# Row scatters of a routed layer: tied by dependences of the transfer in place of waiting GpSimd copies

## The chip, the cores and the metric

The kernel runs on one core of a Trainium2 chip. The metric is the device time of one execution in microseconds: the median of three timed runs before the change is 793.06 us (792.67 to 793.94). A separate, profiled execution shows where the time lies.

Names: PE is TensorE (PEld its weight loads), DVE VectorE, ACT ScalarE, POOL GpSimd, SP SyncE. L634 is line 634 of the kernel before.

## What is computed

The input x has 32 sequences of 256 rows of 128 numbers, all float32. The layer is `x + attention(norm(x)) + experts(norm(x))`:

- attention with 16 heads of 8 numbers, rotated queries and keys, a causal window of 64 positions, softmax, and an output projection;
- a router with 8 experts that keeps two per row with softmaxed weights; each expert is 128 to 512 with gelu, then 512 back to 128.

```
scores = where(j <= i and i - j <= 64, q @ k.T / sqrt(8), -inf)
y = softmax(scores) @ v;  attn = y @ Wproj.T + bproj
weights, indices = top_k(xn @ gate_w.T + gate_b, 2); weights = softmax(weights)
out += w_e * (gelu(xn @ w1[e] + b1[e]) @ w2[e] + b2[e])     for each expert e
return x + attn + out
```

## The kernel before

The order of every engine is the order in which the program is written: all engines are under a manual schedule (L133), and a helper turns data dependences into semaphore waits.

**Attention** runs over 32 sequences z, each in four rounds r = 0 to 3 (L811). A round makes one tile of transposed scores for sequence z on one buffer (`high`, L612: mask matmuls L622, then score matmuls L634) and one tile of the other orientation for an earlier sequence on another buffer (`less`, L681: masks L689, scores L703). VectorE takes the row maxima of the first (mx, L648). ScalarE takes exponentials of the second (pr, L713). Both buffers exist once, so the masks of the next round wait for the maximum and for the exponential. Behind that each round has a job of its own:

- r = 0: values of sequence z - 2 (y, L725), transposed out by VectorE (yt, L734); the parts of the maxima of z - 1 are turned (L672) and copied by ScalarE (L677);
- r = 1: a projection of queries or keys (L549), which VectorE shuffles and multiplies (L558, L565) and GpSimd multiplies for the rotation (L564); the two are added by VectorE two or three rounds later (L571);
- r = 2: more values (L725, L734), the division (L752, L754) and the transpose yT (L760);
- r = 3: the maxima are split into three bfloat16 parts (pc, L659 to L662), v is projected (L589), and the sequence z - 2 ends with the output projection and its addition to x (L774).

**Beside** it a generator (L1037) is advanced once a round by `turn` (L805). It normalises the rows of later sequences (`norm`, L259: statistics on VectorE, the power on GpSimd L274, which is written at the end of the round by `flush`, then the scaling by ScalarE), routes four groups of 16 row tiles (`route`, L306), and writes the row scatters: for each of the 64 tiles of 128 rows and each of the two chosen experts, one indirect DMA from GpSimd that puts 128 rows of 130 numbers (128 values, the row's number and its weight) into the experts' space xs_d in DRAM (`spread_tile`, L454, the DMA at L457). A round has two scatters. `numbers` (L448) writes the row's number and weight into four tiles at a time.

Ahead of each scatter stands a copy of one number on GpSimd (L1079). What it copies is taken from the list `past`, to which the round's VectorE results are appended: the maximum first (L649), then pc (L664), yt (L738), yT (L762) or the sum x (L775). The even scatter's copy reads `past[0]`, the maximum; the odd one's reads `past[-1]`, the last of them. `turn` empties the list (L809). The scatters are declared free of each other (`apart`, L465).

**The experts** (L909) begin when all scatters are written. Attention stands still in between: 71 blocks of 256 rows are loaded by SP (L922 to L932), turned, multiplied up (L952), put through gelu (L958), multiplied down (L970), weighted (L975, L976) and scattered back by GpSimd (L981), each of these scatters with a memset of one number behind it (L988). Then the last ten sequences run through attention while GpSimd adds the experts' rows (L1028).

Of the kernel before, what the change touches and what calls it, by code (L numbers as in the profile page):

```python
# [15 lines left out]
ALU = mybir.AluOpType  # L16
AX = mybir.AxisListType
# [12 lines left out]
NT = TB // P  # L30
# [66 lines left out]
def tile_layer(  # L97
# [16 lines left out]
    nc = tc.nc  # L114
# [12 lines left out]
    def kept(name, shape, dtype=F32):  # L127
        return keep.tile(shape, dtype, tag=name, name=name)
# [18 lines left out]
    xns = [xnp.tile([P, NT, ROW], F32, tag=f"xn{u}", name=f"xn{u}") for u in range(NU)]  # L147
# [43 lines left out]
    xs_d = tc.dram_tile([NE * ER + NI * BT, ROW], F32, name="xs_d")  # L191
# [14 lines left out]
    slot = kept("slot", [P, NN, 2], I32)  # L206
# [238 lines left out]
    spread, returned = [], []  # L445
    gap = kept("gap", [1, 1])

    def numbers(u, k):  # L448

        nc.gpsimd.tensor_copy(  # L450
            xns[u][:, :, D:].bitcast(I32), goes[:, k, u * NT : (u + 1) * NT, :]
        )

    def spread_tile(n, k):  # L454

        spread.append(
            nc.gpsimd.indirect_dma_start(  # L457
                out=xs_d,
                out_offset=bass.IndirectOffsetOnAxis(ap=slot[:, n, k : k + 1], axis=0),
                in_=xns[n // NT][:, n % NT, :],  # L460
                in_offset=None,
            )
        )

    def apart(transfers, name):  # L465

        transfers = [t.ins for t in transfers]
        for t in transfers:
            tc.add_to_no_dep_group(name, t)
        for t in transfers:  # L470
            tc.declare_no_dep(t, group=name, reason="rows of their own")


    class Attention:
# [137 lines left out]
        def high(self, z, m, ip):  # L612

            q, km = self.qk[z // 2, 0][:, z % 2, :], self.kms[z % 3]
            ps = self.ps_s.tile([P, 2, 4, P], F32, tag="sh", name=f"sh{z}_{m}{ip}")

            def masks():
                for ii in range(2):
                    half = slice(HB * ii, HB * ii + HB)
                    for h in range(2):  # L620
                        which = 0 if m == 0 and h == 0 else 1
                        nc.tensor.matmul(  # L622
                            ps[HB * h : HB * h + HB, ii, :, :],
                            lhsT=unit2[half, :],
                            rhs=mq[half, which, :].unsqueeze(1).to_broadcast([HB, 4, 2 * HB]),
                            start=True, stop=False, skip_group_check=True,
                        )

            def scores():
                for h in range(2):  # L630
                    t = 2 * m + h
                    for ii in range(2):
                        r = slice(32 * (2 * ip + ii), 32 * (2 * ip + ii) + 32)
                        nc.tensor.matmul(  # L634
                            ps[HB * h : HB * h + HB, ii, :, :],
                            lhsT=q[r, t * HB : (t + 1) * HB],
                            rhs=km[r, :, t * HB : (t + 2) * HB],
                            start=False, stop=True, skip_group_check=True,
                        )
                        yield  # L640

            def drain():
                if (m, ip) == (0, 0):
                    self.seqs[z] = dict(
                        mx=self.work.tile([P, 2, 4, 4], F32, tag="mx", name=f"mx{z}")
                    )
                mx = self.seqs[z]["mx"][:, m, 2 * ip : 2 * ip + 2, :]
                nc.vector.tensor_reduce(mx, ps, AX.X, ALU.max, negate=True)  # L648
                self.past.append(mx[0:1, 0, 0:1])  # L649

            return masks, scores, drain

        def parts(self, z):

            mx = self.seqs[z]["mx"]
            pc = self.work.tile([P, 2, 4, 4, 3], BF16, tag="pc", name=f"pc{z}")
            at = [pc[:, :, :, :, n].rearrange("p m s i -> p m i s") for n in range(3)]
            rest = self.work.tile([P, 2, 4, 4], F32, tag="rest", name=f"rest{z}")
            nc.vector.tensor_copy(at[0], mx)  # L659
            nc.vector.tensor_sub(rest, mx, at[0])  # L660
            nc.vector.tensor_copy(at[1], rest)
            nc.vector.tensor_sub(at[2], rest, at[1])  # L662
            self.seqs[z]["pc"] = pc
            self.past.append(pc[0:1, 0, 0, 0, 2:3])  # L664

        def parts_rows(self, z, both=False):

# [50 lines left out]
        def values(self, z, n):  # L718

            q = self.seqs[z]  # L720
            py = self.ps_y.tile([P, 4, P], F32, tag="y", name=f"y{z}_{n}")
            for tile_, lo, hi in ((0, 0, P),) if n == 0 else ((2, 0, HB), (1, HB, P)):
                for o in range(2):
                    for i in range(4):
                        nc.tensor.matmul(  # L725
                            py[32 * i : 32 * i + 32, 2 * o : 2 * o + 2, lo:hi],
                            lhsT=self.vsts[z % 3][:, tile_, i, o, :],
                            rhs=q["pr", n, i // 2][:, i % 2, 2 * o : 2 * o + 2, lo:hi],
                            start=True, stop=True, skip_group_check=True,
                        )  # L730

            if n == 0:
                q["yt"] = self.work.tile([P, 4, 8, 32], F32, tag="yt", name=f"yt{z}", bufs=1)
            nc.vector.transpose(  # L734
                q["yt"][:, :, 4 * n : 4 * n + 4, :].rearrange("p s n k -> p s (n k)"), py
            )
            if n == 0:
                self.past.append(q["yt"][0:1, 0, 0, 0:1])  # L738

        def divide(self, z):  # L740

            flat = self.seqs[z]["yt"].rearrange("p s n k -> p (s n k)")
            step = flat.ap[-1][0]

            def view(at, ap):
                return bass.AP(
                    tensor=flat.tensor, offset=flat.offset + at * step,
                    ap=[flat.ap[0]] + [[x * step, y] for x, y in ap],
                )

            rc = self.work.tile([P, 4, 8], F32, tag="rc", name=f"rc{z}")
            nc.vector.reciprocal(rc, view(30, [(248, 4), (32, 8)]))  # L752
            yn = self.work.tile([P, 8, 4, HD], F32, tag="yn", name=f"yn{z}", bufs=1)
            nc.vector.tensor_mul(  # L754
                yn.rearrange("p n s d -> p s n d"),
                view(0, [(264, 4), (32, 8), (1, HD)]),
                rc.unsqueeze(3).to_broadcast([P, 4, 8, HD]),
            )
            yT = self.work.tile([P, T], F32, tag="yT", name=f"yT{z}")
            nc.vector.transpose(yT, yn.rearrange("p n s d -> p (n s d)"))  # L760
            self.seqs[z]["yT"] = yT
            self.past.append(yT[0:1, 0:1])  # L762

        def end(self, z):

            u, b, yT = z // 2, z % 2, self.seqs.pop(z)["yT"]
            po = self.misc(f"pj{z}")
            for n in range(2):
                nc.tensor.matmul(
                    po[:, n * D : (n + 1) * D], lhsT=yT[:, n * P : (n + 1) * P], rhs=wpT,  # L770
                    start=True, stop=True,
                )
            xb = xs[u][:, 2 * b : 2 * b + 2, :]
            nc.vector.tensor_add(xb, po[:, 0 : 2 * D].rearrange("p (n d) -> p n d", d=D), xb)  # L774
            self.past.append(xb[0:1, 0, 0:1])  # L775
            self.ended.add(z)
            if u in self.added:
                self.out(z)
# [85 lines left out]
    att = Attention(list(range(NU)), (work, ps_m, ps_y, ps_s, fixed))  # L864
# [172 lines left out]
    def beside():  # L1037
# [32 lines left out]
        def scatters():  # L1070
            for g in range(NG):
                while g not in slots:
                    yield
                for n in range(2 * GN):
                    k, tile_ = n // GN, g * GN + n % GN
                    if n % NT == 0:
                        numbers(tile_ // NT, k)

                    nc.gpsimd.tensor_copy(gap, att.past[0] if n % 2 == 0 else att.past[-1])  # L1079
                    spread_tile(tile_, k)  # L1080
                    if n % 2:
                        yield

# [8 lines left out]
        def go_on(entry):  # L1092
            entry[2] = next(entry[1], None)
            if entry[2] is None:
# [7 lines left out]
                out=xs_d[rows : rows + NI * BT, :].rearrange("(j p n) d -> p j n d", p=P, n=2),  # L1102
                in_=void[:, 0:NI],
# [3 lines left out]
        u, g, last = 2, 0, False  # L1107
        while next(transfers, transfers) is not transfers:
# [25 lines left out]
            if len(slots) == NG and not last:  # L1134
                begin("blocks", blocks(rt, misc))
                last = True
# [46 lines left out]
```

## Time and profile before

| | |
|---|---|
| median of the timed runs | 793.06 us |
| the profiled execution | 838.41 us, span 836.6 us |
| granted TensorE clock, mean | 0.976 |
| PE, PEld | 750.3 us (90%), 483.2 us (58%) |
| DVE, ACT, POOL | 497.0 us (59%), 381.9 us (46%), 412.0 us (49%) |
| scatters L457 | 128, 126.5 us on POOL, 988 ns each, from 87.9 to 387.3 us |
| copies L1079 | 128 (of mx 80, yt 16, x 16, yT 16), 26.4 us |
| maxima L648 | 128, 156.3 us on DVE, 1221 ns each |
| exponentials L713 | 128, 130.8 us on ACT, 1022 ns each |
| expert scatters L981, memsets L988 | 142 each, 137.3 us and 12.6 us on POOL |

How to read it: busy times are those of one profiled execution. A group's row gives its line, engine, operation and tiles, then busy time and mean duration, then the idle time of its engine just before it and what ended most of that. A row of the waits gives who waited for whom, the total in us, how often, and the longest. In a timeline row the start and duration stand first, and in brackets the idle time before it and its releaser. The ends of matmuls are modelled. By time the execution has four stretches: start and first sequences (to 87 us), attention with scatters (to 387), experts (401 to 673), and the rest of attention (to the end).

### The profile page before, as it was taken

To read this page: it belongs to the slowest core of one execution; us is meant where nothing else is said; L and a number is where in the kernel's file an instruction comes from. 1 tells how busy PE (TensorE), PEld (TensorE's weight loads), DVE (VectorE), ACT (ScalarE), POOL (GpSimd) and SP (SyncE) were. 2 spreads that over 40 slices of the span, in tenths; PEclk is the share of its full clock that TensorE was granted. 3 is DMA by queue.
4 is the path that set the end of the run, shared out by engine and by line. 5 is a ranking of instruction groups with operands and counts; after the bars stand their busy time and mean duration, and the time that the engine had idled before them with its cause. 6 is when DMAs were issued, how large, how long until landed. Compare 5 with 4: busy or idle time off the path is not lost.

```text
span 836.6 us, 20453 instructions
## 1 busy us (share of the span) xinstructions
PE 750.3 (90%) x7524; PEld 483.2 (58%) x7524; DVE 497.0 (59%) x1163; ACT 381.9 (46%) x695; POOL 412.0 (49%) x668
## 2 busy tenths in 40 slices
PE   4899899888888889788999999999999989999985
PEld 2334444444444444333889998999899944444442
DVE  4658867887786687657233333333333348888763
ACT  4346455455455444434434344343344435454552
POOL 2301666477667644664355555555555553634300
PEclk9999999999999999989999999999999999999997
DMA  4600111111111111213677878887778634446100
GB/s 143 179 20 14 46 46 40 46 43 43 49 43 55 50 34 40 96 53 95 199 214 217 224 209 226 227 226 220 219 225 237 198 108 139 137 126 168 41 22 13
DMA packets 126372, 98.87 MB, mean 118 GB/s; under 512 B 14648, under 2 KB 112600, under 8 KB 126272
## 3 DMA queue, kind: packets, MB, share of 16 engines
q1 hardware_dynamic: 117344, 79.64, 34.3%
q0 software_dynamic: 8640, 17.84, 6.1%
q8 instruction: 60, 0.98, 0.5%
q14 instruction: 40, 0.33, 0.1%
q10 hardware_dynamic: 288, 0.08, 0.0%
HBM read 65.09 MB, written 24.02 MB: 107 GB/s over the span
## 4 chain that ended last, share of the span: by engine, by line
PE 63%; ACT 10%; DVE 9%; SPq 7%; issue 6%; DMA 4%; POOL 1%; ACTq 0%; DVEq 0%; POOLq 0%
PE sl L703 10%; PE ph L952 9%; PE po L970 9%; ACT pr L713 9%; PE sl L689 8%; PE sh L634 7%; PE y L725 6%; PE sh L622 5%; DVE mx L648 3%; DMA xg<-xs_d 2%; PE pm L672 2%; PE pk L549 1%; PE pq L549 1%; SPq L932 1%; PE pg L295 1%
## 5 line engine op out<-in xcount | busy, mean ns | idle before, releaser
L713 ACT ACTIVATE pr<-sl 128x1024 f32<-128x1024 f32 x128 | 130.8, 1022 | 232.2 <-PE sh L634 174.2
L648 DVE TENSOR_REDUCE mx<-sh 128x8 f32<-128x1024 f32 x128 | 156.3, 1221 | 106.0 <-PE sh L634 84.7
L981 POOL DMA_INDIRECT ys_d<-yg,at x142 | 137.3, 967 | 138.8 <-DVE yg L976 105.8
L958 ACT ACTIVATE h<-ph,b_b 128x256 f32<-128x256 f32 x284 | 116.3, 470 | 154.6 <-PE ph L952 141.6
L634 PE MATMUL sh<-km,rq 32*64 32x512 f32 x1024 | 153.4, 661 | 0.0
L457 POOL DMA_INDIRECT xs_d<-xn,slot x128 | 126.5, 988 | 44.3 <-issue 27.4
L703 PE MATMUL sl<-qm,rk 32*64 32x256 f32 (+1 forms) x1280 | 147.0, 502 | 0.0
L970 PEld LDWEIGHTS po<-w,h 128*128 128x128 f32 x1136 | 137.9, 192 | 4.3 <-issue 0.7
L970 PE MATMUL po<-w,h 128*128 128x128 f32 x1136 | 138.3, 275 | 0.6 <-issue 0.6
L952 PE MATMUL ph<-xgT,w 128*128 128x256 f32 x568 | 136.2, 383 | 1.1 <-DVE xgT L940 0.9
L689 PE MATMUL sl<-rs,pick_i 76*64 76x512 bf16 x512 | 81.9, 396 | 49.3 <-ACT pr L713 43.6
L952 PEld LDWEIGHTS ph<-xgT,w 128*128 128x128 f32 x568 | 103.3, 192 | 13.0 <-DVE xgT L940 1.1
L975 DVE TENSOR_TENSOR yg<-po,b 128x256 f32<-128x256 f32 x71 | 30.1, 424 | 112.1 <-PE pxg L938 66.4
L725 PE MATMUL y<-pr,vst 128*32 128x128 f32 (+1 forms) x1536 | 78.7, 331 | 2.8 <-issue 1.6
L689 PEld LDWEIGHTS <-pick_i 76*64 76x64 bf16 x512 | 27.8, 109 | 82.8 <-issue 71.2
L725 PEld LDWEIGHTS y<-pr,vst 128*32 128x32 f32 x1536 | 44.8, 117 | 53.3 <-issue 47.4
L703 PEld LDWEIGHTS sl<-qm,rk 32*64 32x64 f32 x1280 | 48.2, 134 | 39.2 <-issue 31.1
L677 ACT COPY rs<-pm 12x1024 bf16<-12x1024 bf16 x63 | 60.2, 1000 | 8.5 <-PE pm L672 7.9
L622 PE MATMUL sh<-mq,unit 64*64 64x512 bf16 x512 | 54.8, 417 | 3.5 <-DVE mx L648 3.2
L734 DVE STREAM_TRANSPOSE yt<-y 128x512 f32<-128x512 f32 x64 | 45.3, 708 | 10.5 <-PE y L725 9.0
L942 DVE COPY at<-xg 128x4 int32<-128x4 int32 x71 | 13.4, 189 | 62.7 <-issue 48.6
L622 PEld LDWEIGHTS <-unit 64*64 64x64 bf16 x512 | 15.7, 105 | 57.5 <-issue 57.2
(143 smaller groups left out, 840.3 us busy)
## 6 DMA issues: line engine op xcount, KB each, us to landing
w<-in_L_ffn_w_dram SPq DMA_DIRECT2D x142, 256.0 KB
xg<-xs_d SPq DMA_DIRECT2D x71, 130.0 KB
yc<-ys_d SPq DMA_DIRECT2D x32, 256.0 KB
b<-b_d SPq DMA_DIRECT2D x71, 64.0 KB
qm<-rq SPq DMA_DIRECT2D x128, 32.0 KB
out_dram<-x SPq DMA_DIRECT2D x32, 128.0 KB
km<-rk SPq DMA_DIRECT2D x126, 32.0 KB
x<-in_L_attn_x_dram SPq DMA_DIRECT2D x15, 256.0 KB
```

Source lines behind the costliest of these rows:

```text
L457: nc.gpsimd.indirect_dma_start(out=xs_d, out_offset=bass.IndirectOffsetOnAxis(ap=slot[:, n, k : k + 1], axis=0), in_=xns[n // NT][:, n % N ...
L622: nc.tensor.matmul(ps[HB * h : HB * h + HB, ii, :, :], lhsT=unit2[half, :], rhs=mq[half, which, :].unsqueeze(1).to_broadcast([HB, 4, 2 * HB]),
L634: nc.tensor.matmul(ps[HB * h : HB * h + HB, ii, :, :], lhsT=q[r, t * HB : (t + 1) * HB], rhs=km[r, :, t * HB : (t + 2) * HB], start=False, ...
L648: nc.vector.tensor_reduce(mx, ps, AX.X, ALU.max, negate=True)
L689: nc.tensor.matmul(ps[HB * e : HB * e + HB, ii, :, :], lhsT=pick_i[:, 2 * ip + ii, :], rhs=rs[e][:, :, n * P : (n + 1) * P], start=True, s ...
L703: nc.tensor.matmul(ps[HB * e : HB * e + HB, ii, :, lo:hi], lhsT=k[r, kt * HB : (kt + 1) * HB], rhs=qm[r, :, n * P + lo : n * P + hi], star ...
L713: nc.scalar.activation(pr, ps, AF.Exp, scale=1.0 / math.sqrt(HD))
L725: nc.tensor.matmul(py[32 * i : 32 * i + 32, 2 * o : 2 * o + 2, lo:hi], lhsT=self.vsts[z % 3][:, tile_, i, o, :], rhs=q["pr", n, i // 2][:, ...
L952: nc.tensor.matmul(ph[:, j * BT : (j + 1) * BT], lhsT=a[:, (k + j) * P : (k + j + 1) * P], rhs=xT, start=True, stop=True,)
L958: nc.scalar.activation(h[:, k + j, :], ph[:, j * BT : (j + 1) * BT], AF.Gelu, bias=b1_b[:, k + j, b : b + 1],)
L970: nc.tensor.matmul(po[:, n, :], lhsT=h[:, k, n * P : (n + 1) * P], rhs=z[:, k, :], start=(k == 0), stop=(k == NHC - 1),)
L981: nc.gpsimd.indirect_dma_start(out=ys_d, out_offset=bass.IndirectOffsetOnAxis(ap=at[:, n, 0:1], axis=0), in_=y[:, n, :], in_offset=None,)
```

## The change

The copies L1079 are gone. `spread_tile` is given an instruction, and the scatter gets a dependence on it with a semaphore, so that the DMA instruction itself waits. `past` now holds two instructions: the round's last score matmul (h and ii both 1) and its maximum. The even scatter waits for the first, the odd one for the second. The other entries of `past` are dropped. Behind each scatter GpSimd now sets one number to zero, as it does behind the experts' scatters.

On TensorE, ScalarE and SP the instructions, their order and their waits are the same as before; on VectorE three of the maxima no longer wait for GpSimd, and nothing else differs. On GpSimd each copy ahead of a scatter becomes a memset behind it, and the order of all else is the same.

```diff
-    def spread_tile(n, k):
+    def spread_tile(n, k, behind):
 
-        spread.append(
-            nc.gpsimd.indirect_dma_start(
...
+        t = nc.gpsimd.indirect_dma_start(
+            out=xs_d,
+            out_offset=bass.IndirectOffsetOnAxis(ap=slot[:, n, k : k + 1], axis=0),
+            in_=xns[n // NT][:, n % NT, :],
+            in_offset=None,
+        )
+        tc.add_manual_dep(
+            t.ins, behind.ins.name,
+            mybir.DependencyInfo(mybir.DependencyClass.Sync, mybir.DependencyReason.DATA),
+            reason="apart",
+        )
+        spread.append(t)
+        nc.gpsimd.memset(gap, 0.0)
...
-                        nc.tensor.matmul(
+                        last = nc.tensor.matmul(
                             ps[HB * h : HB * h + HB, ii, :, :],
...
+                        if (h, ii) == (1, 1):
+                            self.past.append(last)
                         yield
...
-                nc.vector.tensor_reduce(mx, ps, AX.X, ALU.max, negate=True)
-                self.past.append(mx[0:1, 0, 0:1])
+                self.past.append(nc.vector.tensor_reduce(mx, ps, AX.X, ALU.max, negate=True))
...
-            self.past.append(pc[0:1, 0, 0, 0, 2:3])
...
-            if n == 0:
-                self.past.append(q["yt"][0:1, 0, 0, 0:1])
...
-            self.past.append(yT[0:1, 0:1])
...
-            self.past.append(xb[0:1, 0, 0:1])
...
-                    nc.gpsimd.tensor_copy(gap, att.past[0] if n % 2 == 0 else att.past[-1])
-                    spread_tile(tile_, k)
+                    spread_tile(tile_, k, att.past[n % 2])
```

More of the change, by code (lines that the diff above doesn't have):

```diff
@@ L452, in numbers @@
         )
-    def spread_tile(n, k):
-        spread.append(
[L457 to L462, printed above, removed]
-        )
+    def spread_tile(n, k, behind):
[4 more added lines that the diff above has]
+            in_offset=None,
+        )
+        tc.add_manual_dep(
[5 more added lines that the diff above has]
+        nc.gpsimd.memset(gap, 0.0)
     def apart(transfers, name):
```

## The prediction

> **What bounds the kernel now.** I read the page first, then the stretches, then the waits inside the stretch that the change touches. The 128 row scatters run from 87.9 to 387.3 us, so the table of stretches is cut there, with the experts and the attention rounds behind them for comparison. The columns are length, then busy time of PE, weight loads, DVE, ACT and POOL, then clock, DMA share and GB/s.
>
> ```profile
> 87.00:386.00 299.00, 260.09 (x3167) 127.29 (x3163) 223.05 (x521) 144.47 (x229) 190.43 (x315) 0.96 0.15 48
> 401.00:673.00 272.00, 264.88 (x1819) 247.38 (x1820) 95.64 (x278) 116.83 (x284) 145.43 (x276) 1.00 0.76 216
> 690.00:810.00 120.00, 113.10 (x1526) 52.46 (x1524) 95.81 (x156) 59.99 (x81) 47.12 (x37) 1.00 0.38 109
> ```
>
> The experts are bound by TensorE (264.9 of 272 us). The rounds behind them take 120.4/36 = 3.34 us each (from one maximum L648 to the next). The scatter stretch holds 71 rounds in 299 us, 4.21 us each. No engine is full there, so it is a chain of hand-overs. Its waits:
>
> ```profile
> ACT pr L713 <- PE sh L634: 91.5, 43, 3.7
> ...
> DVE mx L648 <- PE sh L634: 43.1, 38, 3.1
> POOL gap L1079 <- DVE mx L648: 37.4, 32, 3.4
> ...
> POOL xs_d L457 <- issue: 27.2, 86, 1.9
> ```
>
> GpSimd waits for the maxima, as the copies demand. ScalarE and VectorE wait for scores, and the timeline shows a part of this that isn't arithmetic. First a round with a scatter, then the same kind of round after the experts:
>
> ```profile
> 252.31 0.59 PE L634 MATMUL sh<-km,rq 32*64 32x512 f32 x1
> 252.34 0.96 POOL L457 DMA_INDIRECT xs_d<-xn,slot  x1 [0.16 <-issue]
> ...
> 253.88 1.23 DVE L648 TENSOR_REDUCE mx<-sh 128x8 f32<-128x1024 f32 x1 [1.34 <-PE sh L634]
> ```
>
> ```profile
> 722.64 0.59 PE L634 MATMUL sh<-km,rq 32*64 32x512 f32 x1
> ...
> 723.33 1.22 DVE L648 TENSOR_REDUCE mx<-sh 128x8 f32<-128x1024 f32 x1 [0.93 <-PE sh L634]
> ```
>
> The last score ends at 252.90 and the maximum starts at 253.88, 0.98 us later, with a scatter running from 252.34 to 253.30. Without a scatter the gap is 723.33 - 723.23 = 0.10. I worked out this lag (start of the maximum less the later of last score's end and VectorE's being free) for all 128 rounds. With a scatter beginning or running around the score's end: 57 rounds, mean 0.67, together 38.0 us. Without: 0.07 (31 rounds) and 0.11 (40 rounds after the experts). The excess is 57 x (0.67 - 0.09) = 33 us, all in this stretch. Hand-overs from VectorE and ScalarE back to TensorE show no such lag.
>
> **How the profiled run stands to the median.** It took 838.4 us (span 836.6), the timed runs 793.1: 45.3 us less. The experts can't shrink by that (TensorE is busy 97%), nor the rounds after them (94%). So most of it must lie in the scatter stretch: 299 - 45 = 254 us, 3.58 a round. Thirteen rounds before and inside that stretch which have norms or routing but no scatter take 3.52; 71 of those are 250 us. Of the 49 us by which the profiled stretch exceeds that, the timed run can then have about 4, a twelfth. This is the number on which I choose: the hold-up is mostly a matter of the profiled execution.
>
> [...] I take the twelfth that the 45 us leave: -2.7 us, bounds 0 and -33.
>
> **The change part by part.** Profile columns: count, busy us, mean ns, then idle time before and its cause.
>
> ```profile
> L457 POOL DMA_INDIRECT xs_d<-xn,slot x127 | 125.5, 988 | 44.2 <-issue 27.2 <-POOL gap L1079 10.6 <-DVE pc L661 1.7
> L1079 POOL COPY gap<-mx 1x1 f32<-1x1 f32 x80 | 17.6, 220 | 38.4 <-DVE mx L648 37.4 <-issue 0.5
> ```
>
> - Removed: 128 copies L1079 (26.4 us on the page) and most of the 44.2 us between a copy and its scatter. Added: 128 memsets at the 88 ns that the same memset behind the expert scatters has (L988): 11.3 us. A scatter behind such a memset starts 0.22 us after it there, and one that waits for VectorE 0.28 us after the result: 128 x 0.25 = 32. GpSimd's use of the stretch is now 190 busy + 44 = 234 us, and after 190 - 26 + 11 + 32 = 207. In the profiled stretch of 299 that is all cover; in 254 us it is 92% before and 81% after. What queues behind a waiting scatter are the rotation products (L564), the power for the norms (L274) and the numbers (L450). VectorE waits for the first two only 0.5 us here, 0 in most rounds. In the tighter timed stretch, 11 norms could each wait up to 1 us: bounds 0 and -11, and since the trace shows almost none I take -1.0.
> - Moved: the even scatter waits for the last score on TensorE instead of the maximum. It now starts a median 0.88 us behind the end of the maximum, some 2.2 us after the score; it will start about 0.3 us after it. The odd one waits for the maximum rather than for the round's last VectorE result; its start goes from a median 2.33 us behind the maximum to some 0.3, if the even one (0.97 us) has ended. Both end some 2.6 us after the score, and the next score ends at 3.3 at the earliest. So maxima and exponentials should no longer be held: that is the -2.7 above. Each wait on GpSimd ends no later than now, so nothing queued behind it gets later.
> - The order on TensorE, VectorE, ScalarE and SP stays as it is; only three maxima lose a wait for GpSimd, which costs nothing today. SP's loads of rows wait for the last scatter: today it ends 387.28 and the first load is issued 388.96. The scatter can end 1.9 us earlier, but SP is itself busy with L580 to 387.2 and then reads two registers, some 1.4 us as between the later loads: -0.3.
> - [...] The even scatter now lies on the reduction, which is good, but in every fourth round the odd one lands on the casts L659 and L661. Rows: the reduction takes 1.22 us with or without a scatter; L659 takes 0.24 us without, 0.30 mean and 0.41 at most with one (8 of 18 have one now). [...] By the row, 8 more casts cost 0.06 to 0.18 each: +0.5, bounds 0 and +2.9.
>
> Sum: -2.7 - 1.0 - 0.3 + 0.5 = -3.5, so 789.5 us. In the profiled execution the whole 33 us are at stake. Against them stand results of values and projections which now meet a scatter: the transposes of y that did so had a lag of 0.25 us (8 cases); 48 rounds x 0.25 = +12. That gives 838.4 - 33 + 12 = about 817 profiled, a far larger fall than in the median.
>
> **Rivals.**
> 1. Slower: the hold-up moves rather than goes. The two scatters fill the 2.6 us behind each score, in which TensorE hands y to L734 and a projection to the rotation (three rounds in four, 48 in all), and VectorE works in order, so a late transpose delays the next maximum. If the hold reaches through both scatters, a transpose starts at about 3.05 instead of 1.3 us: 48 x 1.75 = 84 us against the 33 saved, +51 profiled and, by the twelfth, +4.3 timed: 797, up to 802 if more of it is real. It decides from 33/48 = 0.69 us a hand-over on. For it: the lag of 0.67 for maxima, and holds through two scatters in a row (257.08 to 259.00). Against: y's own rows had 0.25.
> 2. No change: GpSimd's room covers all of it and the timed runs have no hold: 793.0. For it: 45 against 49 us; VectorE almost never waits for GpSimd.
> 3. The hold is real in timed runs and the 45 us lie elsewhere: 33 - 12 = 21 us off, 772. Against: no other stretch has 45 us to give.
> 4. The scatters don't start where they are tied, because GpSimd is still at a rotation (1.27 us) or a power (1.05): then part of them lies as now; it ends between 2 and the forecast.
>
> **How the numbers follow.** Small gain (789.5, 786 to 791.4): 0.38. Rival 1: 0.33. Rivals 2 and 4 (no change): 0.17. Rival 3: 0.12. A difference under 0.2% (1.6 us) can't be told from none. Faster 0.50, same 0.17, slower 0.33. The range runs from 775 (most of rival 3 left out) to 802 (the end of rival 1).
>
> **What would show it.** Right: no L1079 copies; even scatters starting 0.3 us after the last L634; lags of the maxima under 0.2 us in scatter rounds; rounds near 3.8 us; a profiled span near 817 with a median that moves little. Rival 1: L734 and L558 starting 0.7 us or more late behind y and the projections, with TensorE's masks waiting for later maxima. Rival 3: a median falling as much as the span. Wrong altogether: a waiting scatter that costs GpSimd more than 0.3 us each, so that L571 or L278 waits for it.

## The result, and the profile after

The changed kernel takes 803.85 us (median of 11 runs, 798.78 to 811.05), the kernel before 793.06 (11 runs beside it). The two medians by themselves give 1.0136; the recorded ratio, from which one slow run of the changed kernel (811.05 us, at a clock of 0.973) is left out, is 1.0103, 95% interval 1.0075 to 1.0131: **slower by 1.0%**, where a gain of 0.5% was forecast, and above the range of 775 to 802. The changed kernel was run again as an anchor beside later experiments; that gave 1.0097 [1.0073, 1.012], 1.0186 [1.012, 1.0253] and 1.0121 [1.0062, 1.0179].

The profiled execution took 804.07 us (span 802.3, clock 0.982), so this time the profile and the timed runs agree. The kernel before was profiled once more as well (the first experiment): 796.16 us, span 793.4. That execution, and not the one of 838 us, is the partner for a comparison. The stretches of the changed kernel, then those of that second profile of before (columns as above; each first row is about the scatter stretch, the second lies within the experts):

```profile
87.00:365.00 278.00, 256.49 (x3184) 127.30 (x3174) 236.41 (x522) 144.15 (x230) 176.37 (x317) 0.96 0.16 52
380.00:650.00 270.00, 268.19 (x1909) 249.87 (x1907) 97.37 (x280) 118.90 (x284) 148.23 (x284) 1.00 0.76 219
```

```profile
87.00:356.00 269.00, 251.37 (x3168) 124.33 (x3165) 225.60 (x522) 144.48 (x230) 193.50 (x316) 0.97 0.17 54
370.00:640.00 270.00, 267.89 (x1910) 250.06 (x1909) 97.76 (x280) 119.18 (x284) 149.66 (x284) 1.00 0.78 218
```

The experts agree to a few tenths, and so do the last ten sequences (131.2 and 131.1 us from their first maximum to their last). The same work of the first stretch (522 VectorE instructions) takes 9 us more, and VectorE is busy 236.4 us in it instead of 225.6: **10.8 us more for the same instructions**. GpSimd is busy less (176.4 against 193.5, the copies are gone). From the maximum of z = 3, r = 2 to that of z = 21, r = 3, the stretch takes 285.0 us in the changed kernel and 275.5 in before: 9.5 us, against a difference of 8.9 in the whole spans.

The late maxima are gone, as forecast (changed kernel, a round with a scatter; the first row is its last score, which ends at 182.38):

```profile
181.79 0.59 PE L639 MATMUL sh<-km,rq 32*64 32x512 f32 x1
...
182.14 0.96 POOL L456 DMA_INDIRECT xs_d<-xn,slot  x1 [0.21 <-issue]
182.23 0.18 DVE L269 BATCH_NORM_AGGREGATE mv<-st 128x2 f32<-128x6 f32 x1
...
182.49 1.23 DVE L655 TENSOR_REDUCE mx<-sh 128x8 f32<-128x1024 f32 x1
```

The mean lag (from the last score's end, or from VectorE's being free if that is later, to the maximum) in rounds with a scatter is now 0.0 us (38 rounds). But in the second profile of before it is 0.04 (57 rounds): where this kernel takes 794 us, there was nothing to take away. What came instead is seen where one round's chain stretches. The changed kernel, in the round with a projection:

```profile
217.15 0.27 DVE L329 TENSOR_REDUCE t<-oh 128x16 f32<-128x128 f32 x1
...
217.46 1.81 DVE L330 TENSOR_TENSOR oh<-oh,t 128x128 f32<-128x128 f32 x1
217.77 0.09 POOL L468 MEMSET gap<- 1x1 f32 x1
217.82 1.29 POOL L569 TENSOR_TENSOR rotq<-rotq,c 128x512 f32<-128x512 f32 x1
...
219.52 1.21 DVE L655 TENSOR_REDUCE mx<-sh 128x8 f32<-128x1024 f32 x1
```

and the same job in the second profile of before (VectorE's rows):

```profile
209.85 0.27 DVE L329 TENSOR_REDUCE t<-oh 128x16 f32<-128x128 f32 x1
...
210.15 0.29 DVE L330 TENSOR_TENSOR oh<-oh,t 128x128 f32<-128x128 f32 x1
...
211.11 1.23 DVE L648 TENSOR_REDUCE mx<-sh 128x8 f32<-128x1024 f32 x1 [0.34 <-PE sh L634]
```

There the product starts later, at 211.97, under the maximum. In the changed kernel it starts at 217.82, ahead of the maximum; L330 takes 1.81 us instead of 0.29 and ends 0.16 us after the product. The scores ended at 217.98; the maximum, in order behind L330, starts 1.5 us after that, and the masks of the next round wait for it. The rows of two such groups, changed kernel first, then the second profile of before (60 to 366 us):

```profile
L330 DVE TENSOR_TENSOR oh<-oh,t 128x128 f32<-128x128 f32 x8 | 3.9, 488 | 0.3
L323 DVE TENSOR_TENSOR oh<-rest,m 128x128 f32<-128x128 f32 x4 | 3.9, 965 | 0.1
```

```profile
L330 DVE TENSOR_TENSOR oh<-oh,t 128x128 f32<-128x128 f32 x8 | 2.3, 292 | 0.3
...
L323 DVE TENSOR_TENSOR oh<-rest,m 128x128 f32<-128x128 f32 x4 | 1.2, 292 | 0.1
```

I added up, from 60 us to the end of the scatters, how much longer than usual VectorE's instructions take while a rotation product runs: 15.8 us (13 instructions) in the changed kernel, the same within 0.1 in three more profiles of it; 3.3 us (3) in the second profile of before, 1.6 in the first. Such instructions lie on the chain that ended last (the work followed back from the last instruction, at each step to what released it). Changed kernel, six of the ten pieces over 0.85 us (the others: m 0.89, ve 1.01 and 1.06, run 1.10):

```profile
120.85 1.83 DVE off L278
...
154.57 1.69 DVE run L361
...
202.47 1.93 DVE oh L323
...
217.46 1.81 DVE oh L330
...
279.14 1.54 DVE oh L323
...
307.54 1.89 DVE nb_i L389
```

Second profile of before:

```profile
84.87 0.89 DVE m L374
...
285.80 1.09 DVE run L361
...
332.70 2.19 DVE yn L754
```

Ten pieces of 14.8 us stand against three of 4.2. At their usual lengths (ve 0.17, off 0.13, run 0.43, oh 0.29, yn 0.42, the others 0.1) the ten would take 2.4 and the three 1.0, so the chain carries 12.3 us of hold against 3.2: 9.1 us more, about what the stretch grew by.

### The profile page after: what moved, and what is told of

Its sections match the earlier page's. It is cut to its first block, busy times and chain, and to the rows that moved or that the text cites. A ratio compares the mean times of both kernels' runs of the same rounds, so it can differ in the third digit from the quotient of the medians.

```text
span 802.3 us, 20426 instructions
## 1 busy us (share of the span) xinstructions
PE 740.4 (92%) x7524; PEld 480.4 (60%) x7524; DVE 508.9 (63%) x1163; ACT 381.5 (48%) x695; POOL 395.1 (49%) x668
## 4 chain that ended last, share of the span: by engine, by line
PE 65%; DVE 17%; ACT 9%; DMA 3%; issue 3%; SPq 2%; POOL 1%; DVEq 0%; ACTq 0%; POOLq 0%
PE po L971 14%; PE ph L953 14%; PE sl L708 8%; PE sl L694 7%; ACT pr L718 7%; PE sh L639 6%; DVE mx L655 5%; PE sh L627 4%; PE y L730 4%; ACT xn L283 2%; PE pxg L939 2%; PE pg L295 1%; PE pm L677 1%; DMA xg<-xs_d 1%; DVE yt L739 1%
## 5 line engine op out<-in xcount | busy, mean ns | idle before, releaser
L639 PE MATMUL sh<-km,rq 32*64 32x512 f32 x1024 | 151.0, 651 | 0.0
L708 PE MATMUL sl<-qm,rk 32*64 32x256 f32 (+1 forms) x1280 | 144.9, 491 | 0.0
L730 PE MATMUL y<-pr,vst 128*32 128x128 f32 (+1 forms) x1536 | 70.9, 317 | 1.0 <-DVE yt L739 1.0
L730 PEld LDWEIGHTS y<-pr,vst 128*32 128x32 f32 x1536 | 40.2, 110 | 45.0 <-issue 39.8
```

Of the source, the lines that this page charges most:

```text
L639: last = nc.tensor.matmul(ps[HB * h : HB * h + HB, ii, :, :], lhsT=q[r, t * HB : (t + 1) * HB], rhs=km[r, :, t * HB : (t + 2) * HB], start ...
L708: nc.tensor.matmul(ps[HB * e : HB * e + HB, ii, :, lo:hi], lhsT=k[r, kt * HB : (kt + 1) * HB], rhs=qm[r, :, n * P + lo : n * P + hi], star ...
L730: nc.tensor.matmul(py[32 * i : 32 * i + 32, 2 * o : 2 * o + 2, lo:hi], lhsT=self.vsts[z % 3][:, tile_, i, o, :], rhs=q["pr", n, i // 2][:, ...
```

## The experiments

**Theory 1**: the scatters' earlier release lets the rotation products start earlier, among VectorE's instructions that they hold, instead of at the maxima and the transposes behind them. **Theory 2**: the new form costs by itself (a DMA that waits, a memset behind it). Five chips took part, each with the kernel before beside the experiments: A (e0 to e3) 794.3 us, C (f1 to f4) 794.8, D (g1 to g4) 794.3, E (h1, h2) 794.4, but B (e4 to e7) 839.9. Each was used once, so a chip can't be told from its one session. "Held" is the sum defined above, the products' part alone; the expectations count some 1 to 2 us of other holds with it.

**e0: before, once more.** No edit.

> The kernel before, unchanged, profiled a second time. The first profile (838 us) stands 45 us above the median of the timed runs (793), the profile of the changed kernel does not (804 against 804). If profiling a kernel with waiting copies holds TensorE up, the span is near 836 again and the maxima in scatter rounds lag by about 0.67 us. If the first profile was one odd execution, the span is near 791 and the lags are under 0.2 us.

796.16 us, lag of the maxima 0.04 us, held 3.3. The 838 us of the first profile did not come back on this chip.

**e1: the form of the change, at the places of before.** The odd scatter depends on the round's last VectorE result, the even one on the maximum.

```
-                    spread_tile(tile_, k, att.past[n % 2])
+                    spread_tile(tile_, k, att.past[0] if n % 2 == 0 else att.past[-1])
```
(with the results of VectorE in `past` in place of the score)

> The changed kernel's form (the scatter itself waits, a memset behind it), but at the old places: the even scatter behind the maximum, the odd one behind the round's last VectorE result. Theory 1 (the earlier places move GpSimd's rotation products from under the next maximum to where VectorE runs its two-input instructions, which are then held; 15.3 us of held time in the changed kernel's profile against 2.4): about 793, ratio to before 1.00, held time under 4 us. Theory 2 (the form costs: a wait on the DMA instruction or the memsets on GpSimd): about 804, ratio 1.010 to 1.014, whatever the places are.

802.4 us, ratio 1.007 [1.0027, 1.0112]; held 6.7 (under 4 was expected) in its profiled execution, which took 793.6.

**e2: the copies of before, with the memset behind each scatter.**

```
         spread.append(nc.gpsimd.indirect_dma_start(...))
+        nc.gpsimd.memset(gap, 0.0)
```

> The kernel before with its copies, and a memset behind each scatter as well. Adds 128 x 88 ns on GpSimd. Theory 1: within 0.3% of before in time, since places stay. Theory 2: slower by up to 11 us. On the profile: if the missing memset is what let a scatter hold TensorE's results up in the profiled run, the span falls to near 795 and the lags of the maxima go below 0.2 us; if the waiting copies do it, span near 836 and lags near 0.67 stay.

804.9 us, ratio 1.0148 [1.0081, 1.0215], held 5.8. Neither run settles it: both lie between the two kernels or beyond the changed one. A memset of 0.09 us shifts the products too (in e2 they fall on the division, yn 4.4 us), so "form" and "place of the products" can't be separated in this way.

**e3: the products ahead of the round's scatters.**

```
             def turn(z, r):
                 self.now = z, r
+                self.flush(self.past[0] if self.past else None)
                 next(beside, None)
-                self.flush()
```

> The changed kernel, but GpSimd's rotation products and powers are written one round later, ahead of that round's scatters, and wait for that round's last score, so that they run while VectorE takes the maximum. Theory 1: the held VectorE time falls from 15 to under 4 us and the time to that of before or less: 788 to 794, ratio 0.993 to 1.001. Theory 2, or a rival by which the early scatters themselves delay the hand-overs behind a score: 800 to 806, ratio 1.009 to 1.016, or more if scatters now wait behind a product of 1.27 us.

794.9 us, ratio 1.0004 [0.9976, 1.0032]: most of the loss is gone (2.6 us are left at an equal clock, see below), but not for the reason given. The score to which the products were tied was already over, so they started right behind the shuffle, a median 2.0 us before the next maximum, and lay under none (0 of 25 us). Held 8.1 us, but in shorter pieces: those over 0.8 us on the chain are seven of 6.3 us.

**e4 and e5: products that only write.** In the changed kernel (e4, f2) and in before (e5, g2) memsets stand where the product stood; these kernels leave the rotation's second product out of the result:

```
-                self.then(lambda: nc.gpsimd.tensor_mul(rb, rb, sin[:, halves, :]))
+                def work():
+                    nc.gpsimd.memset(rb, 0.0)
+                    nc.gpsimd.memset(rb, 0.0)
+                    nc.gpsimd.memset(rb[:, 0:1, :], 0.0)
+                self.then(work)
```

> The changed kernel with the rotation's product on GpSimd replaced by three memsets of the same tile, together about as long (two whole, one half, estimated 1.3 us from the memsets of 2080, 1280 and 768 numbers at its start, 0.88 ns a number), which write and read nothing. The second product of the rotation is left out of the result. Theory 1 (the products, released earlier, hold VectorE's instructions while they read): the held time of VectorE in the scatter stretch falls from 15 us to under 4, and the time to about that of before or less, 788 to 795. Theory 2 (the new form itself costs: a DMA that waits, a memset behind it, GpSimd's timing): GpSimd is as full as before, so it stays at 800 to 804.

> The control: the same replacement in the kernel before, whose products hold VectorE for only some 3 to 5 us in its profiles. The second product of the rotation is left out of the result. Theory 1: a small gain, 788 to 793, and with the same replacement the changed kernel and this one agree within 3 us. Theory 2: this one about 793, and the changed one some 10 us above it.

These and the next two ran on chip B: 819.0 us (ratio 0.9766 [0.9712, 0.982]) and 835.3 (0.994 [0.9915, 0.9965]). The three memsets took 0.54, 0.53 and 0.31 us in f2, 1.38 together against 1.27 of a product, so GpSimd was no less full.

**e6: even scatter tied to the maximum too. e7: odd scatter tied to the round's last result.**

```
-                    spread_tile(tile_, k, att.past[n % 2])
+                    spread_tile(tile_, k, att.past[1])
```
```
-                    spread_tile(tile_, k, att.past[n % 2])
+                    spread_tile(tile_, k, att.past[n % 2 and -1])
```
(first e6 and f3, then e7 and g1; e7 and g1 with yt, yT, pc and x back in `past`)

> The changed kernel with the even scatter tied to the maximum as the odd one is: the earlier release of the even scatter alone is undone. Theory 1: in the round with the projection the product then starts about 1 us later, behind two scatters that both follow the maximum, nearer to where it was; 793 to 798, held time under 9 us. Theory 2: form and number of instructions are those of the changed kernel, 800 to 804.

> The changed kernel with the odd scatter tied to the round's last VectorE result again (even one at the score): the earlier release of the odd scatter alone is undone. In the round with the projection that last result is the maximum, so the product stays where the change has put it. Theory 1: 799 to 804, held time above 10 us. If the place of the odd scatters (against parts, transposes and casts) were the cause: 793 to 797. Theory 2: 800 to 804.

e6: 845.0 us, ratio 1.0019 [0.9959, 1.0079], held 9.7. e7: 831.2, ratio 0.9896 [0.9867, 0.9926], held 15.1. The times in the expectations hold for a chip of 794 us and say nothing here. Two things do. The held times came out as theory 1 has them: the even scatter's tie moves the products, the odd one's doesn't. And chip B has late maxima. A round of e5 (the last score ends at 216.47):

```profile
215.88 0.59 PE L639 MATMUL sh<-km,rq 32*64 32x512 f32 x1
...
216.10 0.96 POOL L457 DMA_INDIRECT xs_d<-xn,slot  x1 [0.16 <-issue]
...
217.55 1.23 DVE L653 TENSOR_REDUCE mx<-sh 128x8 f32<-128x1024 f32 x1 [1.65 <-PE pq L549]
```

That is the picture of the first profile: lags together 35.4 us in e5 (55 rounds) and 35.3 there by the same count (the prediction has 38.0). With even scatters at the score they fall to 15.5 (e7) and 14.7 (e4); with both scatters at the maximum they stay at 29.4 (e6). The timed runs of that chip are about as long as its profiled ones (e5: a median of 835.3 us, 838.6 profiled), so there the lag isn't made by profiling, and the change's first tie takes more than half of it away.

**f1 to f4: the anchor, and three edits on a chip of 794 us.** f4 multiplies on VectorE:

```
-            if alone:
+            if True:
                 nc.vector.tensor_mul(rb, rb, sin[:, halves, :])
```

> The changed kernel again, as an anchor for the three beside it, because the kernel before took 794 us on the chip of the first four runs and 840 on that of the second four, where its maxima start 0.6 us late in rounds with a scatter (0.04 on the first). Theory 1 as it now stands: the change takes away late maxima where a chip has them (the first profile of before was such an execution), and pays with products that hold VectorE. Where before takes 793: about 803, none of the lag to take away. Where before takes 840: 820 to 830, faster than before, with lags under 0.45 us. The rival (the loss is the form's, on any chip): some 8 us slower than before on either.

> The changed kernel with the rotation's product on GpSimd replaced by memsets of about the same length (the second product of the rotation is left out of the result), as before. Where before takes 793: theory 1 says 788 to 795, the rival 800 to 804. Where before takes 840: some 10 us under the changed kernel beside it by theory 1 (held time 15 us against 2), level with it by the rival.

> The changed kernel with the even scatter tied to the maximum too. Where before takes 793: theory 1 says 793 to 798 (its products hold VectorE for under 9 us), the rival 800 to 804. Where before takes 840: 840 to 847 as measured once, above the changed kernel beside it, since the lag of the maxima (0.54 us in 54 rounds) comes back.

> The changed kernel with the rotation's second product on VectorE, which computes the same in an estimated 0.68 us (as the sum of the same two tiles takes there) instead of 1.24 on GpSimd: 32 x 0.68 = 22 us more of VectorE, against 12 us less of held instructions in the scatter stretch, and no wait between the two engines. Theory 1: below the changed kernel where VectorE has room in that round, 795 to 803 where before takes 793. The rival: above it, by up to 22 us, since nothing is taken away by it.

f1 801.1 us, held 15.9. **f2 790.65 us** (0.9942 [0.9915, 0.9968]); its memsets hold 1.0 us. That is 10.4 us under the anchor (8.1 at an equal clock), with all the DMA waits, the memsets behind them and as full a GpSimd. Theory 2 falls here as the cause of the changed kernel's loss. The two groups shown for the changed kernel have their usual length again in f2:

```profile
L330 DVE TENSOR_TENSOR oh<-oh,t 128x128 f32<-128x128 f32 x8 | 2.3, 292 | 0.3
...
L323 DVE TENSOR_TENSOR oh<-rest,m 128x128 f32<-128x128 f32 x4 | 1.2, 292 | 0.1
```

f3 798.5 us (1.0034 [1.0007, 1.0062]), held 6.6. f4 798.8 (1.0043 [1.0018, 1.0068]), held 0, but each product now takes VectorE 0.69 us: 22 of them in the scatter stretch are 15 us of work against the 15.9 us of hold that are gone.

**g1 to g4.** g3 ties each product to the last score of the next round, ahead of that round's scatters:

```
             def turn(z, r):
                 self.now = z, r
+                for work in self.held:
+                    tc.add_manual_dep(work().ins, self.past[0].ins.name, ...)
+                self.held, self.under = self.under, []
                 next(beside, None)
```
(`project` puts the product into `under` instead of `later`)

> The changed kernel with the odd scatter tied to the round's last VectorE result, the even one to the score. Where before takes 794: theory 1 (products that hold VectorE; held time 13.8 us in its first trace, as much as in the changed kernel) says 799 to 803. If the odd scatter's place in the other three rounds is the larger part of the loss: 793 to 797. Where before takes 840: 831 as before.

> The kernel before with the products replaced by memsets (the rotation's second product is left out of the result). Where before takes 794: theory 1 says 789 to 794, a gain of at most the 4.6 us for which its products hold VectorE. The rival (the products cost the kernel before as much, so that their cost is no matter of the change): 783 to 786, a gain of 8 to 11. Where before takes 840: 835 as before.

> The changed kernel with each product moved one round on, ahead of that round's scatters and tied to that round's last score, so that it starts when the maximum starts (reductions were held in none of 62 overlaps with a product). Nothing is left out. Where before takes 794: theory 1 says held time under 5 us and 789 to 796, level with the kernel whose products only write (790.7), or a few us above it because that round's scatters are 1.3 us later. The rival: 799 to 804. Where before takes 840: under the changed kernel by 6 to 12 us, near 819.

> The changed kernel as an anchor. Where before takes 794: 801 to 804 again. Where before takes 840: theory 1 (late maxima taken away, held instructions added) says 822 to 832, faster than before by 1 to 2%; the rival (the form costs on any chip): 845 to 850.

g1 801.1 us (1.0081 [1.0046, 1.0116]), held 17.4: the odd scatter's tie is no part of the loss. g2 795.2 (1.0001 [0.9976, 1.0026]): the same replacement that gives the changed kernel 10 us gives the kernel before nothing, so the cost is the change's. g3 794.0 (1.0 [0.997, 1.003]), held 1.8, level with before. g4 807.6, above the 801 to 804 expected; its four runs had a mean clock of 0.977.

g3's trace showed 134.2 us for the last ten sequences instead of 131.1. The additions of the experts' rows had moved onto VectorE's parts of the maxima:

```profile
639.98 2.61 POOL L1040 TENSOR_TENSOR x<-x,yc 128x512 f32<-128x512 f32 x2
...
640.52 0.83 DVE L667 CAST pc<-mx 128x32 bf16<-128x32 f32 x1
...
641.38 1.29 DVE L668 TENSOR_TENSOR rest<-mx,pc 128x32 f32<-128x32 f32 x1
```

These two lines together are held 9.3 us there against 2.1 in the changed kernel (L668 takes 0.22 us by itself). h1 therefore moves the products only ahead of the experts.

**h1 and h2: g3 for z below 22, and the anchor.**

```
-                        self.project(u, 1 - z % 2, under=True)
+                        self.project(u, 1 - z % 2, under=z < 22)
```

> The changed kernel with the products moved under the next round's maximum only in the sequences ahead of the experts (z below 22), where the scatters are. Nothing is left out. Where before takes 794: theory 1 says 794 less the 3 us that the last ten sequences lost in the trace of the kernel with all products moved (134.2 us against 131.1): 790 to 792, faster than before, and level with the changed kernel without products that read (790.7). If the moved scatters or products themselves cost what the change gains: 793 to 796. Where before takes 840: near 818.

> The changed kernel as an anchor. Where before takes 794: 801 to 808, as three times so far. Where before takes 840: theory 1 says 822 to 832, faster than before; the rival (the form costs on any chip) 845 to 850.

**h1 takes 792.1 us, ratio 0.9957 [0.9935, 0.998]: 13 us under the changed kernel beside it (7.8 at an equal clock) and 0.4% under before**, with held 1.7; h2 805.4. Whether it is faster than before at an equal clock isn't shown (below). The same job as above, in h1:

```profile
211.39 0.27 DVE L329 TENSOR_REDUCE t<-oh 128x16 f32<-128x128 f32 x1
...
211.70 0.29 DVE L330 TENSOR_TENSOR oh<-oh,t 128x128 f32<-128x128 f32 x1
...
212.37 1.23 DVE L657 TENSOR_REDUCE mx<-sh 128x8 f32<-128x1024 f32 x1
212.42 1.27 POOL L570 TENSOR_TENSOR rotq<-rotq,c 128x512 f32<-128x512 f32 x1 [0.32 <-PE sh L641]
```

The product now starts 0.05 us behind the maximum and outlasts it by 0.09, and neither takes longer.

**How much of these differences is the clock.** Within one kernel the runs' times follow their mean granted clock: a straight line through each kernel's own runs on the chips of 794 us falls 5.9 us per 0.01. By that line, at a clock of 0.987, the changed kernel lies 6.8, 7.4, 7.2 and 7.3 us above before in its four measurements (their raw means 7.6, 6.6, 13.7 and 9.8; the first is set against the runs on chip A, since those beside it have no clock on record), f2 0.7 below, g1 8.2, f4 7.1, f3 4.0, e1 3.7, e3 2.6, g2 1.4 and g3 0.8 above and h1 0.5 below, each to about 1.3 us (2.5 where a kernel has four runs). So the loss stands at an equal clock, while h1's gain goes with a clock of 0.992 against 0.987; whether fewer stalls bring that clock about is left open.

The holds on the chain that ended last, counted in every profile in the same way (pieces held by over 0.3 us, their usual length taken off), put most of the kernels in the same order: 14.4 us in g1, 12.6 to 14.0 in the changed kernel, 6.8 in e3, 6.6 in f3 and e1, 3.3 in before, 1.1 in h1 and g3, 0.8 in f2. Below that of before the times don't follow further: g2 has none and lies 1.4 us above. f4, whose products are on VectorE, can't be set in this row, and e2 (3.4 us on the chain) doesn't fit.

## Why the prediction was wrong, step by step

- **What bounds the kernel** (a chain of hand-overs in the scatter stretch, no engine full): right. All of the change's cost arose there.
- **"The hold-up is mostly a matter of the profiled execution"**: its use was right, its reason not shown. A profile of 796 us, about as long as the timed runs beside it, has none of it (lag 0.04 us), so the first term was about 0 rather than -2.7, within what can be told. No run shows that profiling makes the lag: that profile had none, and chip B shows it in profile (0.64 us in e5) and takes about 840 us in its timed runs too. Which chip the first profile came from isn't on record.
- **Removed and added on GpSimd**: right in size (15 us less were forecast, 17 measured: 193.5 to 176.4 us busy in the two stretches above, the memsets 89 ns), worth nothing. VectorE waited 0.9 us for the power in before; a gain of at most that.
- **"Each wait on GpSimd ends no later than now, so nothing queued behind it gets later": this is the step that failed.** It asks only who is late. The rotation products queue behind the scatters, and they got *earlier*: their median start went from 2.6 us behind the end of the shuffle that feeds them (L558) to 1.2 us, which is from about 1 us after the start of the next maximum to about 1.4 us before it. The term for what queues behind the scatters was put at -1.0; it is about +7 at an equal clock (12.3 against 3.2 us of hold on the chain). f2 and g3 take it away in two ways, and g2 shows that the kernel before has no such loss.
- **The casts beside the odd scatters, +0.5**: a fair figure, weighed in the wrong place. I asked only what the scatters hold, and that was 1.3 us in before and 1.4 to 1.7 after. The GpSimd instruction that VectorE's are held by is the product L569, which the change doesn't touch but moves: 15.8 us in the changed kernel against 3.3 in before. In f2 the memsets, which only write, hold 1.0 us in all. VectorE's products, scans, additions and small scalings of SBUF tiles were held in 133 of 150 overlaps with a product, as counted in the last section; why a product holds them is not shown.
- **Last scatter earlier, -0.3**: 0. The first matmul of the experts follows the last maximum of the stretch by 3.4 us in before and 3.5 after; the load wasn't what it waited for.
- **Rival 1** gave the right sign and 797 us, by another mechanism: no transpose of y was ever held by a product (0 of 101 overlaps), and hand-overs from TensorE had no lag (in the changed kernel's profile a mean of 0.0 us for the maxima of rounds with a scatter, at most 0.1 for the transposes of y). The rivals all asked where a wait would go; none asked what an earlier start would meet.
- **Rival 4** came true in part: the even scatters start a median 0.86 us after the score they wait for, not 0.3, and the odd ones 0.62 us after the maximum's end. 33 of the 64 even ones stand right behind another GpSimd instruction that ended after the score: 18 behind a copy L450, 7 behind a product, 4 behind a power, 4 behind a memset. None of this made the kernel slower by itself: f2 and h1 keep the scatters where the change ties them.
- **Of the profiled 817 us**: it was worked out for an execution with late maxima. The changed kernel wasn't run on such a chip. There the even tie with the products as they are (e7) gave 1.0% and the whole change without reading products (e4) 2.3%, so the changed kernel may well be faster than before on chip B; this is not shown.

What stays open: f3 undoes the even tie and has 4.0 us left at an equal clock, with 3.3 us more of hold on its chain than before; the 0.7 us between them is less than the clock line can tell; e2 has 6.6 us at an equal clock (four runs, to about 2.5) with 5.8 held and no more hold on its chain than before, so its cost is unexplained. The products explain the loss of the changed kernel, and not every figure of its variants.

## What to carry to other kernels

Work that a change lets start earlier is a change too: list what queues behind the released instruction, and look at which instructions of the neighbour engine it will then lie beside. On GpSimd, place a product of two SBUF tiles under a reduction, a transpose or an instruction that reads PSUM (with batch statistics and reciprocals, 0 of 424 overlaps were held in these traces), and not under VectorE's own products, scans and small scalings of SBUF tiles (133 of 150); tie it to the event that starts the cover. And when a profile stands 5% above the timed median, profile the kernel again before building on it; here a second profile came out at 796 us.

## What the runs showed of the hardware

- **VectorE gives way to the rotation products, and they never to it.** In the scatter stretches of all profiles together, VectorE's instructions that overlap a rotation product by 0.1 us or more fall into two classes. Products, scans and additions with both inputs in SBUF, and small scalings and casts in SBUF (ve, m, f), are held to the product's end plus 0.02 to 0.31 us: 133 of 150. The others are 6 that were over when the product had just begun and 11 divisions (yn) that began as it ended. Reductions, batch statistics, transposes, reciprocals and products with a PSUM input: 0 of 424. The product itself takes 1.26 to 1.32 us throughout. Many held instructions have a recorded start up to 0.66 us ahead of the product's (L330 above by 0.36), so here the recorded starts don't tell which of the two is held.
- **GpSimd can be the one that waits.** Its additions of the experts' rows, of the same size and also with two inputs, take 1.26 to 1.29 us when they start under a maximum or a transpose. Begun within a division (yn), they take a median 1.46 us (135 cases in all profiles); begun within the rotation's sum, 1.60 us in five cases. In g3:

```profile
710.32 1.39 DVE L578 TENSOR_TENSOR rq<-rq,rotq 128x512 f32<-128x512 f32 x1
711.24 1.60 POOL L1040 TENSOR_TENSOR x<-x,yc 128x512 f32<-128x512 f32 x1
```

  The sum, itself held by the addition before, ends at 711.71; the addition that began under it ends 0.33 us later than its usual 1.27 us would have it. So in these pairs the one that began later took longer. Why the products show no such case is open.
- **Chips, or their sessions, differ.** Four chips took 794 to 795 us for the kernel before, one 840 (39 runs, 833.7 to 848.4). There the maxima start 0.64 us late in rounds with a scatter (e5's profile; the kernel before itself was not profiled there) instead of 0.04 on chip A. Why a maximum waits through a GpSimd scatter on that chip and not on the others is open.
